# Addend rows of a graph attention layer by VectorE block transpose and two DMAs, with the output store, the values and the setup loads moved

## Chip, cores, metric

One core of one Trainium2 chip. The metric is the device time of that core in microseconds (us), as the median of the runs of one kernel. A single core has no second die to compare with, so a run counts as fast when it is within 1.5% of the fastest run of the same kernel.

## The reference, cut to what matters

64 graphs of 256 nodes, 256 features, fp32. Two layers:

```python
# layer 0: two graph attention (GAT) products, then a feed-forward
def _gat(h, adj, W, a, out_features):
    Wh = jnp.matmul(h, W)
    Wh1 = jnp.matmul(Wh, a[:out_features])
    Wh2 = jnp.matmul(Wh, a[out_features:])
    e = jax.nn.leaky_relu(Wh1 + jnp.swapaxes(Wh2, 1, 2), negative_slope=ALPHA)
    att = jax.nn.softmax(jnp.where(adj > 0, e, NEG), axis=1)
    return jnp.matmul(att, Wh)
h = _gat(_gat(x, adj, W1, a1, Fout), adj, W2, a2, W2.shape[1])
h = _layernorm(x + h, g_ln1, b_ln1)
x = _layernorm(h + relu(h @ w_ff1 + b_ff1) @ w_ff2 + b_ff2, g_ln2, b_ln2)
# layer 1: attention of 8 heads with 4 relations (a mask adj == r and values v_r each),
# output projection Wo, layernorm(x + ...), a feed-forward with gelu, layernorm
```

In each GAT product the sum of a column and a row vector goes through an exponential. The kernel exponentiates the two vectors instead, and needs the row vector (the *addend row*) on all 128 partitions.

## The kernel before

The 64 graphs are worked in 32 pairs. A pair is a Python generator that emits instructions and yields `(us, later, needs)`: how long TensorE's part takes, how much later the next step could go, and which stage it needs for itself. `in_turn` interleaves three pairs by these numbers while the program is built. So the order of instructions on each engine is fixed before the kernel runs.

The addend rows, by eight TensorE transposes (four per graph) and an eviction:

```python
def gat_weights(y, at, rise, ratio, adjT, empty, b):
    p = bank()
    for n in range(4):
        col = rise[:, n // 2, n % 2:n % 2 + 1]
        nc.tensor.transpose(p[:, n * P:(n + 1) * P], col.to_broadcast([P, P]), ident)
    up = work.tile([P, N], F32, name="up", bufs=2)
    nc.scalar.activation(up, p[:, :N], AF.Copy)
    ...                                   # e from p, up, adjT on VectorE; y scaled on ScalarE
```

What VectorE does after the output product of a pair's second GAT layer (the letter `h` further below):

```python
    add_rows(x, ps, b)                    # residual: one 128x512 addition
    layernorm(x, ln[0], b)                # statistics, two scalings per 128 rows
```

The head groups of the attention. A group is four heads of one graph, so a pair has four:

```python
    for n, (b, c) in enumerate(groups):
        ...
        sums(e, po); products(c, 0, v, e, po); products(c, 1, v, ms, po)
        if not last:
            e, ms = ahead, of_relation_1(groups[n + 1][0], ahead)    # VectorE: four masks
        divided(b, c, po)                 # VectorE: reciprocal, range check (junk), oT
        yield 3.1 if last else 4.1, 4.8 if last else 0.8, None
        if (b, c) == (0, KC - 1):         # after the second group
            v = values_tile()
            ...                           # values of the pair's second graph
        if n == 2:
            into_rows(0); yield 1.75, 0.0, None
    into_rows(1)                          # output projection of graph 1: needs the last oT
```

And the end of a pair:

```python
    yield from feed_forward(x, ff1, AF.Gelu, ln[3])
    nc.sync.dma_start(out[...], x)
    yield 3.44, 0.0, None
```

The setup loads pair 0 first, then the weights, and computes small corrections of the biases (matmuls with one column) before pair 0 begins.

## Time and profile before

| | before |
|---|---|
| time, median of the first 3 runs | 3408.89 us (3407.56 to 3410.56) |
| span in the profile | 3408.2 us |
| TensorE / VectorE / ScalarE busy | 98% / 55% / 40% |
| all waits of TensorE | 58.1 us |
| mean granted TensorE clock | 0.993 of full |

The second is where the last GAT product (L277) stands in TensorE's order of time before (start us, us, line, what, count):

```profile
346.64 3.62 PE L339 MATMUL ps<-w_L_gnn_W,ff 128*128 128x256 f32 x16
350.10 1.89 PE L277 MATMUL ps<-xw,e 128*128 128x256 f32 x8
351.82 3.62 PE L339 MATMUL ps<-w_L_gnn_W,ff 128*128 128x256 f32 x16
355.27 1.89 PE L277 MATMUL ps<-xw,e 128*128 128x256 f32 x8
357.00 7.07 PE L339 MATMUL ps<-w_L_gnn_W,ff 128*128 128x256 f32 x32
```

It stands between blocks of another pair's feed-forward (L339). The kernel before works through the GAT layers of three pairs, then through the attention of three pairs. VectorE is busy for 13.6 of the 19 us from 346 to 365 there, but no product of TensorE waits for it.

### The profile page before, as it was taken

To read this page: it belongs to the slowest core of one execution; us is meant where nothing else is said; L and a number is where in the kernel's file an instruction comes from. 1 tells how busy PE (TensorE), PEld (TensorE's weight loads), DVE (VectorE), ACT (ScalarE), POOL (GpSimd) and SP (SyncE) were. 2 spreads that over 40 slices of the span, in tenths; PEclk is the share of its full clock that TensorE was granted. 3 is DMA by queue.
4 is the path that set the end of the run, shared out by engine and by line. 5 is a ranking of instruction groups with operands and counts; after the bars stand their busy time and mean duration, and the time that the engine had idled before them with its cause. 6 is when DMAs were issued, how large, how long until landed. Compare 5 with 4: busy or idle time off the path is not lost.

```text
span 3408.2 us, 46925 instructions
## 1 busy us (share of the span) xinstructions
PE 3341.0 (98%) x18782; PEld 2172.0 (64%) x18782; DVE 1864.6 (55%) x4833; ACT 1366.7 (40%) x2576; POOL 202.9 (6%) x262
## 2 busy tenths in 40 slices
PE   5999999999999999999999999999999999999998
PEld 4666765675576667656756766676576567666755
DVE  3565465645645655656456556556564565565454
ACT  1424523443353255234433532552344335325432
POOL 0000000000000000000000000000000000000000
PEclk7999999999999999999999999999999999999999
DMA  5000100010010001000100100010011001000000
GB/s 162 7 13 25 38 7 7 27 36 7 13 38 19 13 26 38 7 7 30 33 7 13 38 19 13 26 37 7 7 32 31 7 13 38 19 7 19 13 1 14
DMA packets 67297, 78.19 MB, mean 23 GB/s; under 512 B 3713, under 2 KB 58113, under 8 KB 67073
## 3 DMA queue, kind: packets, MB, share of 16 engines
q1 hardware_dynamic: 67072, 75.13, 7.2%
q8 instruction: 150, 2.46, 0.3%
q14 instruction: 75, 0.61, 0.1%
HBM read 58.34 MB, written 16.78 MB: 22 GB/s over the span
## 4 chain that ended last, share of the span: by engine, by line
PE 94%; ACT 4%; DMA 1%; DVE 0%; SPq 0%; issue 0%; POOL 0%; POOLq 0%; DVEq 0%
PE ps L339 26%; PE ps L328 24%; PE ps L362 7%; PE ps L408 6%; PE ps L355 6%; PE ps L380 4%; PE ps L401 4%; PE ps L251 3%; PE ps L425 3%; PE ps L277 3%; PE ps L315 2%; PE ps L265 2%; ACT L213 2%; PE ps L223 1%; ACT L331 1%; ACT xw L267 1%
## 5 line engine op out<-in xcount | busy, mean ns | idle before, releaser
L317 ACT ACTIVATE yT<-ps 128x512 f32<-128x512 f32 x192 | 113.0, 589 | 1057.5 <-PE ps L315 1057.4
L328 PE MATMUL ps<-yT,w_L_gnn_w_ff 128*128 128x512 f32 x1024 | 478.3, 599 | 0.7 <-ACT yT L317 0.7
L328 PE MATMUL ps<-yT,w_L_gnn_W 128*128 128x512 f32 x1024 | 472.5, 596 | 1.4 <-ACT yT L317 1.4
L339 PE MATMUL ps<-w_L_gnn_w_ff,ff 128*128 128x256 f32 x2048 | 456.9, 381 | 0.0
L339 PE MATMUL ps<-w_L_gnn_W,ff 128*128 128x256 f32 x2048 | 456.8, 380 | 0.0
L339 PEld LDWEIGHTS ps<-w_L_gnn_W,ff 128*128 128x128 f32 x2048 | 389.1, 190 | 64.9 <-issue 14.6
L339 PEld LDWEIGHTS ps<-w_L_gnn_w_ff,ff 128*128 128x128 f32 x2048 | 388.0, 190 | 64.5 <-issue 14.3
L394 DVE TENSOR_TENSOR m<-a,adjT 128x512 f32<-128x512 f32 x512 | 327.5, 688 | 175.3 <-ACT a L385 131.1
L300 POOL TENSOR_TENSOR rstd<-rstd,mhalf 128x2 f32<-128x2 f32 x256 | 202.2, 790 | 3198.7 <-DVE rstd L299 3185.0
L385 ACT ACTIVATE a<-ps 128x512 f32<-128x512 f32 x512 | 264.3, 603 | 232.9 <-PE ps L380 232.7
L357 DVE TENSOR_TENSOR v<-ps,b_L_gnn_bv 128x512 f32<-128x512 f32 x128 | 88.2, 689 | 461.4 <-PE ps L355 461.4
L290 DVE TENSOR_TENSOR x<-ps,x 128x512 f32<-128x512 f32 x256 | 176.1, 688 | 262.6 <-PE ps L339 138.9
L331 ACT ACTIVATE ff<-ps,c_L_gnn_b_ff 128x512 f32<-128x512 f32 x256 | 175.9, 687 | 343.2 <-PE ps L328 343.2
L328 PEld LDWEIGHTS ps<-yT,w_L_gnn_W 128*128 128x128 f32 x1024 | 185.6, 190 | 178.7 <-issue 173.5
L328 PEld LDWEIGHTS ps<-yT,w_L_gnn_w_ff 128*128 128x128 f32 x1024 | 182.0, 190 | 177.8 <-issue 175.1
L355 PE MATMUL ps<-wv,yT 128*128 128x512 f32 x512 | 235.4, 592 | 0.0
L331 ACT ACTIVATE ff<-ps,c_L_gnn_b 128x512 f32<-128x512 f32 x256 | 175.7, 686 | 148.3 <-PE ps L328 146.7
L414 DVE RECIPROCAL s<-ps 128x256 f32<-128x256 f32 x128 | 224.2, 1751 | 0.0
L230 DVE SCALAR_TENSOR_TENSOR e<-ps,ratio,up 128x256 f32<-128x256 f32 x256 | 115.9, 477 | 172.6 <-ACT up L225 172.6
L297 DVE BATCH_NORM_STATS2 st<-x 128x6 f32<-128x256 f32 x512 | 192.8, 419 | 8.7
L355 PEld LDWEIGHTS ps<-wv,yT 128*128 128x128 f32 x512 | 97.5, 190 | 122.2 <-issue 122.2
L209 DVE TENSOR_REDUCE steep<-xw 128x1 f32<-128x4 f32 x128 | 19.8, 155 | 254.8 <-ACT xw L267 207.7
(96 smaller groups left out, 4047.9 us busy)
## 6 DMA issues: line engine op xcount, KB each, us to landing
xT<-in_xT SPq DMA_DIRECT2D x32, 512.0 KB, 4.5
adjT<-in_adjT SPq DMA_DIRECT2D x32, 512.0 KB, 3.8
x<-in_x SPq DMA_DIRECT2D x32, 512.0 KB, 4.2
out<-x SPq DMA_DIRECT2D x32, 512.0 KB, 3.2
w_L_gnn_w_ff<-in_L_gnn_w_ff SPq DMA_DIRECT2D x2, 1024.0 KB, 10.4
w_L_gnn_W<-in_L_gnn_W SPq DMA_DIRECT2D x2, 1024.0 KB, 6.9
wv<-in_L_gnn_Wv SPq DMA_DIRECT2D x2, 256.0 KB, 7.4
w_L_gnn_W1T<-in_L_gnn_W1T SPq DMA_DIRECT2D x1, 256.0 KB, 6.1
```

Of the source, the lines that this page charges most:

```text
L290: nc.vector.tensor_tensor(rows, p, rows, ALU.add)
L297: nc.vector.bn_stats(st[:, j, :], r[:, 2 * b + j, :])
L300: nc.gpsimd.tensor_tensor(rstd, rstd, mhalf[:, :2], ALU.pow)
L328: nc.tensor.matmul(p1, lhsT=w1[:, c, m * P:(m + 1) * P], rhs=yT[:, c, :], start=c == 0, stop=c == KC - 1)
L331: nc.scalar.activation(h, p1, func, bias=b1[:, m:m + 1])
L339: nc.tensor.matmul(p2[:, j * D:(j + 1) * D], lhsT=f[m][:, k * P:(k + 1) * P], rhs=w2[:, m, :], start=m == 0, stop=m == NF - 1)
L355: nc.tensor.matmul(ps, lhsT=yT[:, c, at:at + P], rhs=wv[:, c].rearrange("p r m -> p (r m)"), start=c == 0, stop=c == KC - 1)
L362: nc.tensor.matmul(ps, lhsT=w[:, d, c * P:(c + 1) * P], rhs=yT[:, d, :], start=d == 0, stop=d == KC - 1)
L385: nc.scalar.activation(a, ps[o], AF.Exp)
L394: nc.vector.tensor_tensor(m, a, adj, ALU.mult)
L408: nc.tensor.matmul(po[o * DH:(o + 1) * DH, :N], lhsT=v[:, jc, at:at + DH], rhs=ms[o][:, jc * N:(jc + 1) * N], start=r == 0 and jc == 0, st ...
L414: nc.vector.reciprocal(s, po[:, N:])
```

## The change

Its intent: take 512 transposes off TensorE, which is the bound. The addend columns of a pair are written 8 columns apart, transposed in 32x32 blocks by VectorE, stored to DRAM as 4 KB and loaded back onto all partitions as 512 KB. Around that, the schedule leaves more time for this trip; the second graph's values come after the first head group; a pair's output store comes 5 us later; the next pair's loads are asked for one GAT product later (`z` instead of `y` below); the setup loads come in order of need; and the small bias products move to the stage that uses them.

```diff
-        x = io.tile([P, 4, D], F32, name="x", bufs=4)
+        x = io.tile([P, 4, D], F32, name="x", bufs=5)
...
-    loaded = {0: load(0)}                # now after the weights of the first product
...                                       # bias products: relieve(...), called for pair 0 at each stage
-    def addends(y, at, layer, pair, b):
+    def addends(y, at, layer, pair):
...
+        blocks = small.tile([P, 2, 32], F32, name="blocks")
+        nc.vector.transpose(blocks.rearrange("p j c -> p (j c)"), rise.rearrange("p j c -> p (j c)"))
+        row = scratch.tile([2, 16, 32], F32, name="row")
+        nc.sync.dma_start(row.rearrange("j q c -> q j c"), blocks[0:P:8])
+        rows = work.tile([P, 8, 4, 32], F32, name="rows")
+        nc.sync.dma_start(rows.rearrange("p q n c -> p (q n c)"), row.rearrange("j q c -> (j q c)").partition_broadcast(P))
...
-            nc.tensor.transpose(p[:, n * P:(n + 1) * P], col.to_broadcast([P, P]), ident)
...                                       # twice, for the two GAT layers:
+        rows, ratio = addends(y, D + 2, 0, pair)
+        yield 1.75, 8.6, None
+        e = [gat_weights(y, D + 2, rows, ratio, adjT, empty, b) for b in range(2)]
+        yield 0.0, 4.6, None
...
-            if (b, c) == (0, KC - 1):
-                v = values_tile()
+            if n == 0:
+                following = values_tile()
...                                       # the values, then v = following after group 1
         yield from feed_forward(x, ff1, AF.Gelu, ln[3])
+        yield 3.44, 5.0, None
         nc.sync.dma_start(out[...], x)
-        yield 3.44, 0.0, None
```

More of the change, by code (lines that the diff above doesn't have):

```diff
@@ L78, in two_layers @@
     most = const.tile([P, NPAIR, 4], F32, name="most")
-    steep = const.tile([P, NPAIR, 4], F32, name="steep")
+    steep = const.tile([P, NPAIR, 2], F32, name="steep")
+    rises = [const.tile([P, 2, 32], F32, name=f"rise{n}") for n in range(2)]
+    for rise in rises:
+        nc.vector.memset(rise, 0.0)
     def weights(name, pool=const):
@@ L121, in two_layers, with layernorm_weights @@
             nc.vector.tensor_copy(w12[:, m], pw[:, :D + 4])
-    ln = [tuple(on_all(n, D) for n in names) for names in (
-        ("L0_gnn_g_ln1", "L0_gnn_b_ln1"), ("L0_gnn_g_ln2", "L0_gnn_b_ln2"),
-        ("L1_gnn_g1", "L1_gnn_beta1"), ("L1_gnn_g2", "L1_gnn_beta2"))]
+    loaded = {0: load(0)}
+    def layernorm_weights(g, beta, more=None):
+        return on_all(g, D), on_all(beta, D), more and (on_all(more, D), column(more + "c"))
+    ln = [layernorm_weights("L0_gnn_g_ln1", "L0_gnn_b_ln1", "L0_gnn_b_ff2")]
     ff0 = (weights("L0_gnn_w_ff1"), column("L0_gnn_b_ff1"), weights("L0_gnn_w_ff2"))
-    wq, wk, wo = weights("L1_gnn_Wq"), weights("L1_gnn_Wk"), weights("L1_gnn_Wo")
+    ln.append(layernorm_weights("L0_gnn_g_ln2", "L0_gnn_b_ln2", "L1_gnn_bo"))
+    wq, wk = weights("L1_gnn_Wq"), weights("L1_gnn_Wk")
     wv = const.tile([P, KC, 2, D], F32, name="wv")
@@ L133, in two_layers @@
     bq, bk, bv = column("L1_gnn_bq"), column("L1_gnn_bk"), on_all("L1_gnn_bv", 2 * D)
+    bqs = const.tile([P, KC], F32, name="bqs")
     nc.vector.tensor_tensor(bv[:, D:], bv[:, D:], bv[:, :D], ALU.subtract)
+    wo = weights("L1_gnn_Wo")
+    ln.append(layernorm_weights("L1_gnn_g1", "L1_gnn_beta1", "L1_gnn_b2"))
     ff1 = (weights("L1_gnn_W1"), column("L1_gnn_b1"), weights("L1_gnn_W2"))
-    bqs = const.tile([P, KC], F32, name="bqs")
-    with tc.tile_pool(name="setup", bufs=1) as setup, \
-            tc.tile_pool(name="psetup", bufs=2, space=bass.MemoryType.PSUM) as psetup:
-        for n, (name, readers) in enumerate((("L0_gnn_b_ff2", ((ff0[0], ff0[1]),)),
-                                             ("L1_gnn_bo", ((wq, bq), (wk, bk))),
-                                             ("L1_gnn_b2", ((ff1[0], ff1[1]),)))):
-            beta = ln[n][1]
-            nc.vector.tensor_tensor(beta, beta, on_all(name, D, setup), ALU.add)
-            b = setup.tile([P, KC], F32, name="c_" + name)
-            nc.sync.dma_start(b, t[name + "c"])
-            for w, bias in readers:
-                pw = psetup.tile([P, 512], F32, name="pw")
-                of = w.shape[-1] // P
-                for m in range(of):
-                    for c in range(KC):
-                        nc.tensor.matmul(pw[:, m:m + 1], lhsT=w[:, c, m * P:(m + 1) * P], rhs=b[:, c:c + 1],
-                                         start=c == 0, stop=c == KC - 1)
-                nc.vector.tensor_tensor(bias, bias, pw[:, :of], ALU.subtract)
-            if name == "L1_gnn_bo":
-                pw = psetup.tile([P, 512], F32, name="pw")
-                for c in range(KC):
-                    nc.tensor.matmul(pw, lhsT=b[:, c:c + 1].to_broadcast([P, P]),
-                                     rhs=wv[:, c].rearrange("p r m -> p (r m)"), start=c == 0, stop=c == KC - 1)
-                nc.vector.tensor_tensor(bv, bv, pw, ALU.subtract)
-        nc.vector.tensor_scalar(bqs, bq, SCALE, None, ALU.mult)
@@ L162, in two_layers @@
+    ln.append(layernorm_weights("L1_gnn_g2", "L1_gnn_beta2"))
+    for gbm in ln[:3]:
+        nc.vector.tensor_tensor(gbm[1], gbm[1], gbm[2][0], ALU.add)
     work = ctx.enter_context(tc.tile_pool(name="work", bufs=1))
     small = ctx.enter_context(tc.tile_pool(name="small", bufs=6))
+    scratch = ctx.enter_context(tc.tile_pool(name="scratch", bufs=4, space=bass.MemoryType.DRAM))
     psum = ctx.enter_context(tc.tile_pool(name="psum", bufs=8, space=bass.MemoryType.PSUM))
@@ L167, in bank, with relieve, relieve_attention @@
         return psum.tile([P, 512], F32, name="ps")
+    def relieve(bias, w, more):
+        p = bank()
+        of = w.shape[-1] // P
+        for m in range(of):
+            for c in range(KC):
+                nc.tensor.matmul(p[:, m:m + 1], lhsT=w[:, c, m * P:(m + 1) * P], rhs=more[1][:, c:c + 1],
+                                 start=c == 0, stop=c == KC - 1)
+        nc.vector.tensor_tensor(bias, bias, p[:, :of], ALU.subtract)
+    def relieve_attention(more):
+        relieve(bq, wq, more)
+        relieve(bk, wk, more)
+        nc.vector.tensor_scalar(bqs, bq, SCALE, None, ALU.mult)
+        p = bank()
+        for c in range(KC):
+            nc.tensor.matmul(p, lhsT=more[1][:, c:c + 1].to_broadcast([P, P]),
+                             rhs=wv[:, c].rearrange("p r m -> p (r m)"), start=c == 0, stop=c == KC - 1)
+        nc.vector.tensor_tensor(bv, bv, p, ALU.subtract)
     alone = {}
@@ L202, in of_graph, with gat_weights @@
         return slice(2 * b, 2 * b + 2)
-    def addends(y, at, layer, pair, b):
-        k = of_graph(b)
-        nc.vector.tensor_reduce(steep[:, pair, 2 * layer + b:2 * layer + b + 1], y[:, k, at:at + 2], axis=AX.XY,
-                                op=ALU.max, apply_absolute_value=True)
-        e1, e2 = y[:, k, at], y[:, k, at + 1]
-        rise, ratio = small.tile([P, 2, 2], F32, name="rise"), small.tile([P, 2], F32, name="ratio")
-        nc.scalar.activation(rise[:, 0], e1, AF.Exp, bias=shift[:, 0:1])
-        nc.scalar.activation(rise[:, 1], e1, AF.Exp, bias=shift[:, 0:1], scale=ALPHA)
-        nc.scalar.activation(ratio, e2, AF.Exp, scale=ALPHA - 1.0)
-        return rise, ratio
-    def gat_weights(y, at, rise, ratio, adjT, empty, b):
-        p = bank()
-        for n in range(4):
-            col = rise[:, n // 2, n % 2:n % 2 + 1]
-            nc.tensor.transpose(p[:, n * P:(n + 1) * P], col.to_broadcast([P, P]), ident)
-        up = work.tile([P, N], F32, name="up", bufs=2)
-        nc.scalar.activation(up, p[:, :N], AF.Copy)
+    def addends(y, at, layer, pair):
+        nc.vector.tensor_reduce(steep[:, pair, layer:layer + 1], y[:, :, at:at + 2], axis=AX.XY, op=ALU.max,
+                                apply_absolute_value=True)
+        rise, ratio = rises[layer], small.tile([P, 4], F32, name="ratio")
+        of_kind = rise.rearrange("p j (n s) -> p n j s", n=4)[:, :, :, 0]
+        for b in range(2):
+            e1 = y[:, of_graph(b), at]
+            nc.scalar.activation(of_kind[:, 2 * b], e1, AF.Exp, bias=shift[:, 0:1])
+            nc.scalar.activation(of_kind[:, 2 * b + 1], e1, AF.Exp, bias=shift[:, 0:1], scale=ALPHA)
+        nc.scalar.activation(ratio, y[:, :, at + 1], AF.Exp, scale=ALPHA - 1.0)
+        blocks = small.tile([P, 2, 32], F32, name="blocks")
[4 more added lines that the diff above has]
+        nc.sync.dma_start(rows.rearrange("p q n c -> p (q n c)"), row.rearrange("j q c -> (j q c)").partition_broadcast(P))
+        return rows, ratio
+    def gat_weights(y, at, rows, ratio, adjT, empty, b):
         e = work.tile([P, 2, N], F32, name="e", bufs=4)
@@ L229, in gat_weights @@
             k = 2 * b + j
-            nc.vector.scalar_tensor_tensor(e[:, j], p[:, N:], ratio[:, j:j + 1], up, op0=ALU.mult, op1=ALU.max)
+            nc.vector.scalar_tensor_tensor(e[:, j].rearrange("p (q c) -> p q c", q=8), rows[:, :, 2 * b + 1],
+                                           ratio[:, k:k + 1], rows[:, :, 2 * b], op0=ALU.mult, op1=ALU.max)
             nc.vector.scalar_tensor_tensor(e[:, j], adjT[:, k], empty[:, k:k + 1], e[:, j],
@@ L244, in gat_layers @@
         z = work.tile([P, 4, D + 4], F32, name="xw", bufs=2)
-        a, e = [], []
         for b in range(2):
@@ L253, in gat_layers @@
                 nc.scalar.activation(y[:, k], ps[:, :D + 4], AF.Copy)
-            a.append(addends(y, D + 2, 0, pair, b))
-            yield 1.75, b * 1.6, None
-        if pair + 1 < NPAIR:
-            loaded[pair + 1] = load(pair + 1)
-        for b in range(2):
-            e.append(gat_weights(y, D + 2, *a.pop(0), adjT, empty, b))
-            yield 0.5, b * 4.4, None
+            if b == 0:
+                yield 1.75, 0.0, None
+        rows, ratio = addends(y, D + 2, 0, pair)
+        yield 1.75, 8.6, None
+        e = [gat_weights(y, D + 2, rows, ratio, adjT, empty, b) for b in range(2)]
+        yield 0.0, 4.6, None
         for b in range(2):
@@ L267, in gat_layers @@
                 nc.scalar.activation(z[:, 2 * b + i, :D + 2], ps[:, :D + 2], AF.Copy)
-            a.append(addends(z, D, 1, pair, b))
-            yield 1.75, 0.4 + b * 0.6, None
-        for b in range(2):
-            e.append(gat_weights(z, D, *a.pop(0), adjT, empty, b))
-            yield 0.5, b * 4.4, None
+            if b == 0:
+                yield 1.75, 0.4, None
+        rows, ratio = addends(z, D, 1, pair)
+        if pair + 1 < NPAIR:
+            loaded[pair + 1] = load(pair + 1)
+        yield 1.75, 8.6, None
+        e += [gat_weights(z, D, rows, ratio, adjT, empty, b) for b in range(2)]
+        yield 0.0, 4.6, None
         for b in range(2):
@@ L292, in layernorm @@
     def layernorm(r, gb, b):
-        g, beta = gb
+        g, beta, _ = gb
         st, mv = small.tile([P, 2, 6], F32, name="st"), small.tile([P, 2, 2], F32, name="mv")
@@ L455, in attention @@
             yield 3.1 if last else 4.1, 4.8 if last else 0.8, None
-            if (b, c) == (0, KC - 1):
-                v = values_tile()
+            if n == 0:
+                following = values_tile()
                 for jc in range(2):
-                    values(v, jc, N + jc * P, yT)
+                    values(following, jc, N + jc * P, yT)
                     yield 1.72, 0.0, None
+            if n == 1:
+                v = following
             if n == 2:
@@ L471, in whole_way @@
         yield from gat_layers(pair, xT, adjT, x)
+        if pair == 0:
+            relieve(ff0[1], ff0[0], ln[0][2])
         yield from feed_forward(x, ff0, AF.Relu, ln[1])
         yield 3.44, 6.0, None
+        if pair == 0:
+            relieve_attention(ln[1][2])
         yield from attention(x, pair, adjT)
+        if pair == 0:
+            relieve(ff1[1], ff1[0], ln[2][2])
         yield from feed_forward(x, ff1, AF.Gelu, ln[3])
+        yield 3.44, 5.0, None
         nc.sync.dma_start(out[2 * pair:2 * pair + 2].rearrange("b (c p) d -> p (b c) d", p=P), x)
-        yield 3.44, 0.0, None
     in_turn((whole_way(pair) for pair in range(NPAIR)), 3)
-    ranges = ((reach, NPAIR * 4, N * SAFE), (most, NPAIR * 4, 1.0), (steep, NPAIR * 4, STEEP))
+    ranges = ((reach, NPAIR * 4, N * SAFE), (most, NPAIR * 4, 1.0), (steep, NPAIR * 2, STEEP))
     count = const.tile([P, len(ranges)], F32, name="count")
```

## The prediction

> **What bounds the kernel now.** I read the page's busy shares first, then TensorE's own waits, TensorE's groups by shape, the start in order of time, and one stretch in the middle.
>
> ```profile
> PE 3341.0 (98%) x18782; PEld 2172.0 (64%) x18782; DVE 1864.6 (55%) x4833; ACT 1366.7 (40%) x2576; POOL 202.9 (6%) x262
> ```
>
> TensorE is the bound and the others are near half. A busy share of 98% could hide waits, so the next view is who TensorE waited for (engine, line, releaser: us in total, times, longest):
>
> ```profile
> PE ps L223 <- ACT rise L213: 19.4, 23, 0.9
> PE pw L151 <- DMA b_L_gnn_bo<-in_L_gnn_bo: 18.9, 1, 18.9
> PE pw L119 <- DVE junk L113: 11.4, 1, 11.4
> PE ps L265 <- ACT xw L236: 2.9, 1, 2.9
> PE ps L277 <- ACT xw L236: 2.6, 1, 2.6
> ```
>
> All eight rows of that view add to 58.1 us in 3408. 30.3 of them are two waits at the start (L119, L151). The L265 and L277 waits are the first pair's, which has no company. From 78 us on, TensorE waits almost only for L223, the transposes that spread the addends; 20 of those waits are 0.92 us each, two in every batch of three pairs (ScalarE has just reloaded its table between Gelu and Exp). So the time is the sum of TensorE's own work plus the start, and only what leaves TensorE's queue counts.
>
> What L223 costs, from TensorE in order of time in the middle (start, us, line, what, count):
>
> ```profile
> 328.26 1.04 PE L223 MATMUL ps<-ident,rise 128*128 128x128 f32 x8
> 329.13 1.88 PE L328 MATMUL ps<-yT,w_L_gnn_W 128*128 128x512 f32 x4
> ```
>
> The 1.04 includes the pipeline's tail; the next group starts 0.87 us after the first. Eight transposes (one layer of one pair) hold TensorE for 0.87 us, 109 ns each, not the 273 ns that the group's mean shows.
>
> The start:
>
> ```profile
> 11.41 3.50 PE L119 MATMUL pw<-right,w_L_gnn_W1T 128*128 128x260 f32 x8 [11.41 <-DVE junk L113]
> ...
> 33.81 6.96 PE L151 MATMUL pw<-c_L_gnn_b_ff,w_L_gnn_w_ff 128*128 128x1 f32 x32 [18.90 <-DMA b_L_gnn_bo<-in_L_gnn_bo]
> ...
> 54.67 5.80 PE L251 MATMUL ps<-w,xT 128*128 128x260 f32 x16 [0.25 <-DVE c_L_gnn_b L153]
> ```
>
> The first useful product of pair 0 (L251) starts at 54.67 us although its own inputs are ready near 15.4 us (the second copy into w12 starts at 14.95 and takes 0.43). It is held behind the tiny bias products, 33.81 to 54.5 us, which wait for nearly all weights.
>
> **What the Trainium skill says.**
> 1. "TensorE: Matmul & The Clock Gate", Back-to-back issue gap: spacing, not duration, sets throughput; it gives about 81 ns per matmul of 128 columns. The trace agrees in kind, with 109 ns for these fp32 transposes beside a duration of 273 ns.
> 2. "DMA: Bandwidth & Descriptors", Anatomy of one DMA: a fixed cost of about 2 us plus bytes over 436 GB/s. For 512 KB that is an estimate of 3.2 us; the trace has 3.2 us (out), 3.8 (adjT) and 4.5 (xT). The page's fit is for the other descriptor path, but the sizes match here.
> 3. The same page, Two DMAs through the same engine are not ordered: a DMA that reads what another wrote must wait for its completion. So the new store and load cost two full latencies in series. No run yet shows it.
> 4. "VectorE: DVE Perf Modes", The three transpose paths: the VectorE transpose works in 32x32 blocks only. That is why the change spaces the columns and sends the row through DRAM. The trace before has no such instruction.
>
> **The change part by part.**
> *Transposes.* Removed: 32 pairs x 2 layers x 8 = 512 transposes on TensorE, 64 x 0.87 = 55.7 us, and their waits, 19.4 us. Both are on the path. Sum 75.1 us. Also removed: 128 ScalarE evictions of 0.38 us (49 us, beside other work, worth nothing).
> Added per pair and layer: one VectorE transpose of 128x64, taken as about 0.15 us as the small VectorE instructions are; a 4 KB store; a 512 KB broadcast load. 64 loads are 33.5 MB, at some 280 GB/s (what the start moves: 9.1 MB of loads in some 33 us) 120 us of DMA time spread over 3400: bandwidth is free. Latency is the question. From the end of a layer's products to the next matmul: eviction 0.39, two exponentials 0.58, VectorE transpose and hand-over 0.3, store 0.45 issue + about 2.0 (skill), load 0.4 + 3.8 (adjT row), two pairs of scalar_tensor_tensor 1.9, reciprocal 0.16, two scalings 0.9: 10.9 us, with one table load (1.28) 12.2. The schedule asks for 8.6 + 4.6 = 13.2 us of other work, more after rounding up to whole steps of 1.72 or 3.44 us. TensorE has it: while one pair is in these layers another is in a feed-forward (27.5 us of products: 8 x 1.72 + 4 x 3.44), and a third follows it. Now the two gaps are 7.6 and 10.4 us and cost only the 0.9 above. The slack is 1 to 3 us; the next pair's xT load (512 KB) becomes free exactly when the first layer's products end and can delay that layer's store by 2 us. I allow 8 us of new waits in all: some 10 batches, 0.8 us each.
> *Start.* The four setup loads no longer queue behind 1.5 MB of pair 0: at 280 GB/s 5 us, less some issue, so L119 can start near 7.5 and L251 near 12, 42 us earlier. But pair 0 now needs two store-and-load trips with nothing beside them, and the first queues behind the remaining loads, which the old kernel was issuing until 36.5 us. I estimate the first rows at 44 to 49 us, the second layer's products at 48 to 52, the third (L277) at 63 to 67 instead of 74.4. The 20.7 us of tiny products are not saved; they move. If they fall into the idle stretch of pair 0 the start gains some 8 to 12 us; if they stay after it in TensorE's order, the start loses about 10. VectorE's L240 for pair 3 runs at 61 us, far ahead of its place in the program, so instructions are moved forward when they can run: I give the first case 0.7. Expected gain 4 us.
> *Second graph's values earlier, x with five buffers, output store 5 us later.* No product is added or removed, and TensorE waits for none of these now: 0 us. They protect the queue that now carries the rows.
> Sum: 3408.9 - 75.1 - 4 + 8 = 3337.8; new waits are as likely near nothing, so I put the point at 3335.
>
> **The rivals.**
> *The DMA trip becomes the wait.* If a trip takes 3 us more than reckoned, every L265 or L277 in steady state waits some 1 to 2 us: 62 x 1.5 = 93 us, and the gain is gone (3400 or so). For it: the slack is thin, and stores, xT loads and rows now share one queue. Against it: transfers are only 7.2% of the engines' time, output stores of 512 KB land in 3.2 us, and the 8.6 looks fitted to such a trip. A weaker form, 20 us, gives 3350.
> *The start eats part.* Pair 0 alone pays two trips behind 9 MB of loads and the tiny products come later: +10 to +15 us instead of -4, so 3350.
> *VectorE or ScalarE as bound.* 55% and 40% busy, and ScalarE loses work: no.
> *Start goes well.* Rows sent before the prefetches, trips hidden: 20 us more, 3315.
>
> **Range and chances.** Removal of 75 us is firm; start (-20 to +15) and new waits (0 to 25) are not. Eight in ten: 3316 to 3360. 2% faster means under 3340.7, just above my point, so faster 0.57, within 2% 0.42, slower 0.01.
>
> **What would show it.** Right: no transpose group of L223's kind left and 18270 or so TensorE matmuls; TensorE's waits for the scaled rows (L265 and L277's successors) under 10 us after the start; the rows' load landing in about 4 us; L251's first start near 12 us. Wrong: waits of 1 us or more repeating at the same place of each batch, DVE waiting for the DMA of the rows for longer than the 13 us of cover, or the tiny products running after pair 0's L277 in time.

## More of the kernel before

TensorE's order in the traces was the order of the program.

The prediction shows most of what is to be read. Two more readings are needed for what follows. The first is the page's chain that ended last, before, as shares of the span:

```profile
PE 94%; ACT 4%; DMA 1%; DVE 0%; SPq 0%; issue 0%; POOL 0%; POOLq 0%; DVEq 0%
```

VectorE (DVE) has no part in it.

## The result and the profile after

A ratio below is the mean time of one kernel's fast runs over that of the other's in the same rounds, so it is not quite the ratio of the medians that stand beside it. Its interval is the 95% one.

| | before | after |
|---|---|---|
| time, median of 4 runs | 3408.22 us (3406.43 to 3410.56) | 3387.49 us (3387.21 to 3388.09) |
| ratio | | 0.994 [0.9925, 0.9955] |
| span in the profile | 3408.2 us | 3385.3 us |
| mean granted TensorE clock | 0.993 | 0.991 |

The change is 0.6% faster. The prediction said 3335 us, 3316 to 3360; the kernel is outside, on the slow side. The busy shares and the chain of the page after:

```profile
PE 3288.2 (97%) x18270; PEld 2108.3 (62%) x18270; DVE 1841.2 (54%) x4835; ACT 1262.0 (37%) x2326; POOL 203.1 (6%) x262
...
PE 83%; DVE 11%; DMA 3%; POOL 1%; issue 1%; ACT 0%; SPq 0%; POOLq 0%; DVEq 0%
```

The transposes are gone: 512 matmuls fewer, 18782 - 18270. The chain now runs through VectorE for 11% of the span, although VectorE's busy share fell from 55 to 54%. What TensorE waited for, after (engine, line, releaser: us in total, times, longest):

```profile
PE ps L437 <- DVE oT L430: 40.9, 30, 2.1
PE ps L274 <- ACT xw L247: 28.3, 1, 28.3
PE ps L289 <- ACT xw L247: 9.1, 1, 9.1
PE pw L121 <- DVE junk L115: 7.5, 1, 7.5
```

L274 and L289 are the GAT products that need the rows. Each waited once in the whole run, for pair 0. So the trip through DRAM is hidden in the steady state. The new wait is L437: the output projection waits for `oT`, the attention's divided result, once in nearly every pair. Neither instruction is in a changed line.

One such wait, after, in TensorE's order of time:

```profile
430.61 1.99 PE L289 MATMUL ps<-xw,e 128*128 128x256 f32 x8
...
441.73 1.05 PE L420 MATMUL ps<-m,v 128*32 128x256 f32 x16
442.71 0.66 PE L327 MATMUL ps<-ident,x 128*128 128x128 f32 x4
...
445.36 3.62 PE L351 MATMUL ps<-w_L_gnn_W,ff 128*128 128x256 f32 x16
448.81 0.59 PE L437 MATMUL ps<-w_L_gnn_Wo,oT 128*128 128x256 f32 x2
451.10 1.56 PE L437 MATMUL ps<-w_L_gnn_Wo,oT 128*128 128x256 f32 x6 [1.69 <-DVE oT L430]
```

The last head group's products end near 442.7. TensorE has 6.1 us of other work (442.71 to 448.81) before the output projection of graph 1 comes up, and stops after its first two matmuls. What VectorE did in that time, after, in order:

```profile
443.27 0.68 DVE L302 TENSOR_TENSOR x<-ps,x 128x512 f32<-128x512 f32 x1
...
444.97 1.22 DVE L251 TENSOR_REDUCE most<-adjT 128x4 f32<-128x1024 uint32 x1
...
447.69 0.88 DVE L318 SCALAR_TENSOR_TENSOR x<-x,rstd,b_L_gnn_beta 128x256 f32<-128x256 f32 x2 [0.58 <-POOL rstd L312]
448.49 1.75 DVE L426 RECIPROCAL s<-ps 128x256 f32<-128x256 f32 x1
...
450.63 0.42 DVE L430 TENSOR_TENSOR oT<-ps,s 128x256 f32<-128x256 f32 x1
```

The reciprocal of the last group (L426) had its inputs near 442.8; it starts at 448.49, 5.7 us later. Ahead of it in VectorE's queue stand the addition and layernorm of output projection 0, and a reduction of the next pair (L251). They themselves stand late, because earlier in the same attention VectorE had to do the addition and layernorm of both GAT products: L289 at 430.61 is the second of them, between head groups. The same place before, TensorE and VectorE in order of time:

```profile
306.52 7.17 PE L339 MATMUL ps<-w_L_gnn_W,ff 128*128 128x256 f32 x32
...
309.09 1.75 DVE L414 RECIPROCAL s<-ps 128x256 f32<-128x256 f32 x1
...
313.53 1.89 PE L425 MATMUL ps<-w_L_gnn_Wo,oT 128*128 128x256 f32 x8
```

There the last group's products end at 306.6 and the reciprocal starts 2.5 us later. TensorE has 7.0 us of other work (306.52 to 313.53), so the result, done at 311.65, is in time. The change adds 3.2 us to VectorE's delay and takes 0.9 us of work from in front of the projection.

The load of the two stretches, in one view: window, then busy us (instructions) of TensorE, its weight loads, VectorE, ScalarE and GpSimd, the granted clock, DMA share and GB/s. Both begin just before the first head group and end just after the last output projection. Before:

```profile
282.00:317.00 35.00, 35.00 (x313) 21.85 (x307) 26.15 (x52) 14.67 (x20) 1.58 (x2) 1.00 0.06 17
```

and after:

```profile
418.00:453.00 35.00, 33.31 (x315) 20.82 (x308) 29.51 (x64) 9.94 (x17) 2.38 (x3) 1.00 0.05 16
```

VectorE is busy for 26.15 of 35 us (75%) before, 29.51 us (84%) after. Over the whole run it is 55% and 54%: the average hides the place where TensorE waits. (The 60% in two expectations below is of 270 to 305 us before, which begins 12 us earlier in the attention; the like stretch after, 406 to 441, has 23.41 of 35 us, 67%.)

The order that does this, as matmul calls of one pair (read from the program; `y z h` GAT products: input, second, output; `F f` feed-forward first and second product; `q` projections, `v` values, `s` scores, `u p` sums and products of a head group, `o` output projection):

```
before, three pairs in turn through  y8 F8 z4 F2 z4 F6 f8 h4 f8 h4 f16,  then three through
        F10 q4 v2 s8 q4 v2 s8 u8 p16 F2 s8 u8 p16 F2 v4 s8 u8 p16 F2 o4 u8 p16 f16 o4 f16
after,  one pair at a time through
        q4 v2 s8 q4 v2 s8 u8 p16 h4 v4 s8 u8 p16 h4 s8 u8 p16 F2 o4 u8 p16 F2 f8 o4 f24
        F6 y8 F10 f16 z4 f8 z4 f8 F12
```

The `h4` that stood between feed-forward blocks stand between head groups now. The last output projection has `F2 f8` ahead of it instead of `f16`.

The start, after, all engines in order of time:

```profile
30.13 0.58 SPq L229 DMA_DIRECT2D row<-blocks  x1
36.60 0.34 SPq L231 DMA_DIRECT2D rows<-row  x1
...
43.96 6.37 PE L274 MATMUL ps<-xw,e 128*128 128x258 f32 x16 [28.33 <-ACT xw L247]
...
59.44 5.44 PE L289 MATMUL ps<-xw,e 128*128 128x256 f32 x16 [9.11 <-ACT xw L247]
...
68.22 3.63 PE L162 MATMUL ps<-c_L_gnn_b_ff2c,w_L_gnn_w_ff 128*128 128x1 f32 x32
...
73.52 10.37 PE L340 MATMUL ps<-yT,w_L_gnn_w_ff 128*128 128x512 f32 x20 [0.74 <-ACT yT L329]
```

Pair 0's first row was ready to store near 16.8 us, when its VectorE transpose ended; the store is issued at 30.13, after SyncE (SPq) has issued all remaining setup loads. Still, the first feed-forward product (L340) starts at 73.52, and at 85.66 before.

Where the 22.9 us between the two spans come from, by TensorE's time from one matmul's start to the next one's, with the waits counted apart:

| term | us |
|---|---|
| transposes gone, 61.2, and their waits, 19.4 | -80.6 |
| waits at the start: 11.4 + 18.9 before, 7.5 after | -22.8 |
| bias products: 20.6 before, 10.5 after | -10.1 |
| pair 0's waits for its rows: 28.3 + 9.1, against 2.9 + 2.6 | +31.9 |
| other matmuls, mostly the first product of layer 0's feed-forward (448.0 to 441.3) | -5.0 |
| GAT products spaced wider | +13.4 |
| L437: 40.9 of waits, and 9.4 to drain and refill | +50.3 |
| sum | -22.9 |

The rows of -5.0 and +13.4 belong together. Matmuls right behind a head group's narrow products are spaced wider. Before, these are feed-forward products (14.15 us for a pair's 32, against 13.74 where none of them stands there); after, GAT products (1.88 us for eight, against 1.73). The granted clock is 1.00 in both stretches above.

### The profile page after: what moved, and what is told of

Same layout as the page of the kernel before. It is cut to its first block, busy times and chain, and to the rows that moved or that the text cites. A ratio compares the mean times of both kernels' runs of the same rounds, so it can differ in the third digit from the quotient of the medians.

```text
span 3385.3 us, 45656 instructions
## 1 busy us (share of the span) xinstructions
PE 3288.2 (97%) x18270; PEld 2108.3 (62%) x18270; DVE 1841.2 (54%) x4835; ACT 1262.0 (37%) x2326; POOL 203.1 (6%) x262
## 3 DMA queue, kind: packets, MB, share of 16 engines
q1 hardware_dynamic: 79360, 108.95, 10.2%
## 4 chain that ended last, share of the span: by engine, by line
PE 83%; DVE 11%; DMA 3%; POOL 1%; issue 1%; ACT 0%; SPq 0%; POOLq 0%; DVEq 0%
PE ps L340 24%; PE ps L351 23%; PE ps L374 7%; PE ps L367 6%; PE ps L420 4%; PE ps L392 4%; PE ps L274 3%; PE ps L261 3%; DVE s L426 3%; PE ps L413 3%; PE ps L289 2%; DVE m L406 2%; DMA adjT<-in_adjT 2%; PE ps L327 2%; PE ps L437 2%; DVE x L318 2%
## 5 line engine op out<-in xcount | busy, mean ns | idle before, releaser
L340 PE MATMUL ps<-yT,w_L_gnn_W 128*128 128x512 f32 x1024 | 471.6, 597 | 0.7 <-ACT yT L329 0.7
L340 PE MATMUL ps<-yT,w_L_gnn_w_ff 128*128 128x512 f32 x1024 | 452.0, 594 | 0.7 <-ACT yT L329 0.7
L340 PEld LDWEIGHTS ps<-yT,w_L_gnn_w_ff 128*128 128x128 f32 x1024 | 192.6, 191 | 217.5 <-issue 207.7
L340 PEld LDWEIGHTS ps<-yT,w_L_gnn_W 128*128 128x128 f32 x1024 | 183.7, 190 | 185.7 <-issue 178.1
L240 DVE SCALAR_TENSOR_TENSOR e<-rows,ratio 128x256 f32<-128x256 f32 x256 | 116.1, 476 | 273.9 <-DMA rows<-row 249.4
L426 DVE RECIPROCAL s<-ps 128x256 f32<-128x256 f32 x128 | 223.6, 1747 | 0.0
L437 PE MATMUL ps<-w_L_gnn_Wo,oT 128*128 128x256 f32 x512 | 130.5, 389 | 40.9 <-DVE oT L430 40.9
```

The lines of the kernel that those rows point to most:

```text
L340: nc.tensor.matmul(p1, lhsT=w1[:, c, m * P:(m + 1) * P], rhs=yT[:, c, :], start=c == 0, stop=c == KC - 1)
L426: nc.vector.reciprocal(s, po[:, N:])
L437: nc.tensor.matmul(ps[:, j * D:(j + 1) * D], lhsT=oT[:, c, k * P:(k + 1) * P], rhs=wo[:, c, :], start=c == 0, stop=c == KC - 1)
```

## The experiments

The theory from the result, called A: the longer trip and the 5 us moved the GAT output products into the attention, VectorE falls behind there, and the last output projection pays. The rival B: moving the values behind the first group overloads VectorE, or makes the wait by its own order. Beside them stands the question of what the rows and the start are worth alone. Each kernel ran four times, in three sets of four kernels on one chip each; the kernel before had 7 runs in each set, with medians 3409.71, 3408.85 and 3410.45, so the sets can be compared to about a microsecond. All results were correct.

**1. values_back: the values at their old place.**

```diff
-            if n == 0:
-                following = values_tile()
+            if (b, c) == (0, KC - 1):
+                v = values_tile()
...
-            if n == 1:
-                v = following
```

> The changed kernel with the second graph's values put back behind the second head group. Theory A (the longer trips and the later end of a pair push the second layer's outputs h, with their residual add and layernorm on VectorE, between the head groups of the pair before; VectorE falls behind and the last output projection waits for oT): the order of h within the head groups stays, so some 30 waits of 1 to 2 us stay and the time is 3380 to 3395. Rival B (the values, 3.4 us of TensorE work that used to stand between the second and third head group, gave VectorE its breath, and moving them made the wait): the waits vanish and the time falls to 3335 to 3350.

Measured 3441.04 us (3438.47 to 3445.72), ratio 1.0097 [1.0081, 1.0114]. TensorE's largest wait there:

```profile
PE ps L420 <- DVE v L369: 66.1, 47, 2.4
```

B's forecast of a faster kernel falls: in this order the early values save 54 us (3441.0 - 3387.5). At the old place the values' bias additions queue up on VectorE behind the GAT layernorm, and the products wait for them. About half of the 54 us is this waiting (66.1 us against 40.9). The rest is in the products of the head groups, which take some 27 us more by the count of the account: after the waits the granted clock falls (0.76 from 439 to 446 us; over the run 0.981, against 0.991). The L437 wait is gone from the list; TensorE stops earlier, which gives VectorE time. So the values' place decides where TensorE stops, and B is right in that.

**2. store_back: the store at once, as before.**

```diff
-        yield 3.44, 5.0, None
         nc.sync.dma_start(out[...], x)
+        yield 3.44, 0.0, None
```

> The changed kernel with the output store issued at once and no 5 us delay at a pair's end. In the program's own order the pairs then go in batches of three again and no h stands between head groups. Theory A: TensorE's wait for oT falls from 40.9 us to under 10, VectorE's busy share inside the attention stretch falls from 84% to near 60%, time 3332 to 3350. Rival B: the values still stand early, so the waits stay and the time is over 3375. Rival C (the trips of the rows through DRAM cost TensorE time once their cover shrinks): new waits of L274 or L289 of 1 us and more per pair, time over 3360.

Measured 3372.76 us (3369.88 to 3374.97), ratio 0.9892 [0.9876, 0.9909]: 15 us better than after, between what A and B forecast. In the program's order the pairs go in batches of three again, and only one of three has its `h4` in the attention. That pair pays:

```profile
PE ps L437 <- DVE oT L430: 15.9, 10, 2.7
```

10 times, at most once per batch: 2.70 us four times, 0.96 us five times, 0.3 us once. So the late end is what brought the GAT products into *every* pair's attention; the longer trip alone brings them into one of three. I had taken the late end for the whole cause.

**3. cover: more time declared between the last head group and its output projection.**

```diff
-            yield 3.1 if last else 4.1, 4.8 if last else 0.8, None
+            yield 3.1 if last else 4.1, 8.0 if last else 0.8, None
```

> The changed kernel with 8.0 instead of 4.8 us asked for between the last head group and its output projection: one more feed-forward step (3.4 us) stands between, h stays between the head groups. Theory A and rival B alike: the wait for oT (1 to 2 us each) is covered, waits under 5 us, time 3335 to 3350. Rival D (the time is lost in something else, such as the switching of TensorE between small and full matmuls): the wait goes but the time falls by less than 20 us.

Measured 3344.88 us (3344.65 to 3348.45), ratio 0.9815 [0.9798, 0.9831]; the interval straddles 2%. The order differs from the kernel after only in that one feed-forward block more stands ahead of the last `o4` (`f16 o4 f16` for `f8 o4 f24`). In TensorE's order of time:

```profile
444.16 7.07 PE L351 MATMUL ps<-w_L_gnn_W,ff 128*128 128x256 f32 x32
451.07 1.89 PE L437 MATMUL ps<-w_L_gnn_Wo,oT 128*128 128x256 f32 x8
```

The eight matmuls of L437 run without a stop and the wait is gone from the whole list. It returns 42.6 us (3387.5 - 3344.9) of the 50.3 in the account; one new wait of 5.5 us at the end of the run (at 3301 us, where the last pair has no company) takes back most of the rest. VectorE's load in the same window is the same or higher, 30.46 of 35 us. The last reciprocal is as late as in the kernel after (5.6 us): its group's products end at 441.6, it starts at 447.17. So the 50 us are not a lack of VectorE time as such, but of 3.4 us of other work at one place. A and B expected this alike: the run shows what the wait costs, not what makes it. Rival D falls.

**4. rows_by_pe: the transposes back, the rest of the change kept.**

```diff
+        for n in range(4):
+            nc.tensor.transpose(p[:, n * P:(n + 1) * P], col.to_broadcast([P, P]), ident)
-        nc.sync.dma_start(row.rearrange("j q c -> q j c"), blocks[0:P:8])
-        nc.sync.dma_start(rows.rearrange("p q n c -> p (q n c)"), ...)
...                                       # and the yields of the GAT layers and the next pair's load as before
```

> The changed kernel with the addend rows made by the old TensorE transposes, all else as changed. Theory A: without trips the second layer is early enough, no h between head groups, no wait for oT (under 5 us), but 512 transposes are back (61 us of TensorE and some 18 us of waits): 3395 to 3408, so start and the rest alone gain 0 to 12 us against the kernel before. Rival B: the wait for oT stays (30 x 1.5 us) and the time is 3430 to 3450.

Measured 3374.85 us (3374.47 to 3376.63), ratio 0.9899 [0.9882, 0.9915]: 20 to 33 us faster than expected, and 12.6 us *faster than the whole change*. So within this change the new rows cost more than they save. The rest of the change gains 34 us without them: pair 0 has its transposes and no trip, and its first feed-forward product starts at 52.7 us.

**5. first_pe_cover: cover, and the transposes for pair 0 alone.**

```diff
+        if pair == 0:
+            return rise, ratio            # no trip
...
+        if by_transposes:                 # pair 0
+            for n in range(4):
+                nc.tensor.transpose(p[:, n * P:(n + 1) * P], rows[:, n % 2, at_n:at_n + 1].to_broadcast([P, P]), ident)
...
-            yield 3.1 if last else 4.1, 4.8 if last else 0.8, None
+            yield 3.1 if last else 4.1, 8.0 if last else 0.8, None
```

> The kernel with 8.0 us of cover, and pair 0 alone makes its addend rows by the old TensorE transposes; pairs 1 to 31 by the two DMAs. If the trips of pair 0 (behind the remaining loads, with nothing beside them) are what costs the start, TensorE's waits of 27.0 and 9.4 us before pair 0's second and third products shrink to some 3 us each, the first feed-forward product comes near 53 us instead of 74, and the time falls by 18 to 24 us from 3345, to 3320 to 3328. If the start is held by the loads of the weights instead, the time stays over 3338.

Measured 3320.68 us (3319.3 to 3323.83), ratio 0.9742 [0.9726, 0.9758]. This beats both kernels: 2.6% faster than before. Its start, TensorE in order of time:

```profile
22.36 3.75 PE L286 MATMUL ps<-xw,e 128*128 128x258 f32 x16 [2.63 <-ACT xw L259]
...
30.86 5.33 PE L301 MATMUL ps<-xw,e 128*128 128x256 f32 x16 [3.29 <-ACT xw L259]
...
47.55 10.55 PE L352 MATMUL ps<-yT,w_L_gnn_w_ff 128*128 128x512 f32 x20 [0.74 <-ACT yT L341]
```

The first feed-forward product starts 26 us earlier than after (73.52), and 24.2 us are gained over cover.

**6. more_dve: one spare 128x512 addition on VectorE after each GAT layernorm.**

```diff
             layernorm(x, ln[0], b)
+            spare = work.tile([P, 512], F32, name="spare")
+            nc.vector.tensor_tensor(spare, x[:, of_graph(b), :]..., x[:, of_graph(b), :]..., ALU.add)
```

> The changed kernel with one more VectorE addition of 128x512 (about 0.69 us, its result unused) after each graph's layernorm of the second layer, that is two per pair between the head groups; TensorE's order is unchanged. Theory A (VectorE's queue is the last to arrive at the output projection): the wait for oT grows by 1.0 to 1.4 us per pair, from 40.9 us to 70 to 85, time 3415 to 3430. Rival E (the wait is the latency of the last division alone, whatever VectorE did before): unchanged within 5 us, 3382 to 3392.

Measured 3445.84 us (3439.07 to 3448.65), ratio 1.0103 [1.0086, 1.0119]: 58 us slower than after, more than expected, although the L437 wait (here L440) grew less than expected, from 40.9 to 62.8 us. That is 22 of the 58. Most of the rest shows in TensorE's order of time:

```profile
454.56 0.59 PE L440 MATMUL ps<-w_L_gnn_Wo,oT 128*128 128x256 f32 x2
458.22 2.93 PE L440 MATMUL ps<-w_L_gnn_Wo,oT 128*128 128x256 f32 x6 [3.07 <-DVE oT L433]
```

The same six matmuls that took 1.56 us after a wait of 1.69 take 2.93 us after a wait of 3.07. The window after it, in the columns given above, has a granted clock of 0.61:

```profile
458.00:462.00 4.00, 3.78 (x11) 3.14 (x12) 0.94 (x3) 0.00 (x0) 0.00 (x0) 0.61 0.00 0
```

So a wait can cost its own time and then a stretch of 3.4 us at half the granted clock. That followed 14 of the 18 waits of over 2 us here. Between 80 and 3300 us such stretches add up to 51.2 us here and 10.2 us in the kernel after; half of the difference, some 20 us, is the loss (an estimate). A's direction is confirmed.

**7. rows_only: only the rows, in the kernel before.** The diff is the `addends`, `gat_weights` and GAT yields of the change, on the kernel before; nothing else.

```diff
-            nc.tensor.transpose(p[:, n * P:(n + 1) * P], col.to_broadcast([P, P]), ident)
+        nc.sync.dma_start(row.rearrange("j q c -> q j c"), blocks[0:P:8])
+        nc.sync.dma_start(rows.rearrange("p q n c -> p (q n c)"), ...)
...
+        yield 1.75, 8.6, None
```

> The kernel before with nothing changed but the addend rows (VectorE transpose, two DMAs, the delays that go with them); start, values, output store and buffers as before. In the program's order the pairs stay in batches of three and no h stands between head groups. Theory A: no wait of the large kind, at most one wait for oT in three pairs; of the 80 us of transposes and their waits some 18 are paid back in pair 0's two trips and some 25 in waits: 3370 to 3385. If the rows by DMA are no gain in themselves (rival C): over 3400.

Measured 3372.58 us (3371.17 to 3375.88), ratio 0.9894 [0.9877, 0.991], as expected. The rows alone gain 36 us of the 75 that I had reckoned. Pair 0's two trips wait 10.4 and 9.6 us there, and one pair of three has its `h4` in the attention.

**8. values_only: only the values early, in the kernel before.**

```diff
-            if (b, c) == (0, KC - 1):
-                v = values_tile()
+            if n == 0:
+                following = values_tile()
...
+            if n == 1:
+                v = following
```

> The kernel before with nothing changed but the second graph's values, moved behind the first head group. No h stands between head groups there, so VectorE is at 60% and neither place makes a wait: 3405 to 3412, no wait for oT or v of over 0.5 us. If the early values alone made the wait for oT: 3440 or more.

Measured 3409.05 us (3407.14 to 3410.23), ratio 0.9997 [0.9981, 1.0014]. In the old order the move is worth nothing, as the prediction said, and there is no wait for `oT`. Experiment 1 shows that this does not carry over to the new order.

**9. less_dve: the range check of the divided groups taken out.** The kernel guards itself with it; it is left out on purpose here. The results stay right for these inputs, but the guard is gone.

```diff
-            nc.vector.scalar_tensor_tensor(junk, po[:, N:], 1.0, s, op0=ALU.mult, op1=ALU.add,
-                                           accum_out=reach[:, pair, b * KC + c:b * KC + c + 1])
```

> The changed kernel without the range check that VectorE makes in each division (one scalar_tensor_tensor of 128x256 and its accumulator read, about 0.42 us in the queue, four per pair; the checked value is set to 1 once, so the guard is gone on purpose while the output stays right). TensorE's order is unchanged, h still stands between the head groups. Theory A: VectorE arrives 1.3 to 1.7 us earlier at the last division, the wait for oT falls from 40.9 us to under 8, time 3335 to 3350. If the wait were made by TensorE's order or by a DMA: unchanged, 3380 or more.

Measured 3358.19 us (3354.36 to 3360.1), ratio 0.9845 [0.9829, 0.9862]. The wait for `oT` fell to 15.5 us in 29 waits, from 40.9 in 30. Half a microsecond of VectorE work less per group returns 29 us: the direction of A again, with a gain smaller than expected.

**10. first_pe: the transposes for pair 0 alone, without cover.** The diff is that of experiment 5 without its last two lines.

> The changed kernel with pair 0's addend rows by TensorE transposes and nothing else: the start and the waits for oT are separate, so it gains what it gained beside the cover (24 us): 3360 to 3368, with the wait for oT still near 41 us.

Measured 3364.21 us (3358.98 to 3364.58), ratio 0.9861 [0.9844, 0.9877]. The start gains 23.3 us and the wait for `oT` stays, 40.6 us. The two repairs add up: 23.3 + 42.6 = 65.9, and both together gained 66.8 (3387.5 - 3320.7).

**11. start_only: only the order of loads and the bias products, in the kernel before.**

```diff
-    loaded = {0: load(0)}
...
+    loaded = {0: load(0)}                 # after the weights of the first product
...
+        if pair == 0:
+            relieve(ff0[1], ff0[0], ln[0][2])
...                                        # and so at the two other stages
```

> The kernel before with the changed start alone: loads in order of need, pair 0's loads behind the four setup loads, the tiny products in front of the stage that needs them; rows by TensorE transposes, values, output store and buffers as before. If the start alone is what made the kernel with the old transposes 35 us faster: 3370 to 3380. If the later output store had a part in it: 3385 or more.

Measured 3385.38 us (3385.01 to 3387.03), ratio 0.9929 [0.9913, 0.9946]. The start is worth 25 us when pair 0 need not make the trip; it alone does not make the 34 us of experiment 4 (the second case of the expectation). That leaves about 10 us of the 34 of experiment 4 for the rest. The traces put them mostly with the later end of a pair: TensorE's waits for the transposes are 19.4 us in 23 waits here and 10.2 in 13 in experiment 4. No run has the later end alone, so that share is a reading.

**12. store_values_back: rows and start, with values and store at their old places.** The diffs of 1 and 2 together.

> The changed kernel with the output store and the second graph's values both put back: the pairs go in batches of three, no h between head groups, and the values stand between the second and third group. It is the kernel with the rows alone (3372.6) plus the changed start, which is worth some 14 us beside pair 0's two trips (35 less 21): 3353 to 3364, waits for oT under 5 us. If the early values cost nothing in this order, as in the kernel before: the same as with the store alone put back, 3370 to 3376.

Measured 3359.71 us (3357.2 to 3362.86), ratio 0.9854 [0.9838, 0.9871], as expected. With it the four kernels that have the new rows and the new start make a table (medians, us):

| | values at the old place | values early |
|---|---|---|
| store at once | 3359.7 | 3372.8 |
| store 5 us later | 3441.0 | 3387.5 |

The later store costs 81 us or 15 us; the early values cost 13 us or save 54 us. Neither move has a worth of its own; each changes what stands in VectorE's queue when the other acts. With the store at once, the wait for `oT` is 15.9 us with early values and 1.5 us without: it takes both, the GAT products in the attention and the early values, for the stop to be at L437. Without both, this change would have been 28 us faster than it was.

## Why the prediction was wrong

**Transposes.** Right, and a little small: 75.1 us reckoned, 80.6 in the account. Eight of them took 0.96 us on average (61.2 / 64), not 0.87.

**The trip.** Right. The rows' load was to land in about 4 us and the row store in about 2:

```profile
rows<-row SPq DMA_DIRECT2D x64, 512.0 KB, 3.7
...
row<-blocks SPq DMA_DIRECT2D x64, 4.0 KB, 2.2
```

The VectorE transpose took 0.24 us; 0.15 was assumed. After pair 0 TensorE never waits for L274 or L289. The rival that feared most for this trip did not come about, and none of the 8 us allowed for new waits was of that kind.

**The skill's statements.** "DMA: Bandwidth & Descriptors", Anatomy of one DMA, gave an estimate of 3.2 us for 512 KB, by a fit for another descriptor path; measured 3.7. Two DMAs through the same engine are not ordered, of the same page, agrees: the load waited for the store's completion in each of its 64 uses, 113.2 us in all, 1.8 us each. "VectorE: DVE Perf Modes", The three transpose paths: the 32x32 blocks are why the columns stand apart, and that worked.

**The start.** Its sum was near, its parts were not. L121 at 7.50 and L261 at 11.86 came as reckoned. The rows' products came at 43.96 and 59.44, earlier than the 48 to 52 and 63 to 67 estimated. "Instructions are moved forward when they can run" did not hold on TensorE: the bias products stand where the program has them, at 68.22, after pair 0's L289. (On VectorE it did: pair 3's first instruction, L251, runs at 48.30.) This was the case to which the prediction gave 0.3 and a loss of 10 us. It cost less, because the bias products run at full clock now: 32 of them in 3.63 us at a granted clock of 1.00, against 6.96 us at 0.50 before. From the account the start and the trips sum to -22.8 - 10.1 + 31.9 = -1.0 us, and -4 was predicted; that the two are near is luck. A pair 0 without trips would have made it some 23 us better (experiment 10).

**The step that failed** is two sentences: "TensorE waits for none of these now: 0 us", for values, buffers and store, and "VectorE or ScalarE as bound. 55% and 40% busy, and ScalarE loses work: no". Also "while one pair is in these layers another is in a feed-forward" was read from the old order and taken for the new. The `yield` numbers that were to hide the trip, and the 5 us at the end of a pair, are inputs of a schedule that is laid out again from them. It put the GAT output products into the attention. There VectorE went from 75 to 84% busy, its last reciprocal started 5.7 instead of 2.5 us after its inputs, and one matmul group in nearly each pair waited 1.4 us on average (40.9 / 30). The wait and the refill are 50.3 us, and the spacing of the other products 13.4 - 5.0 = 8.4 more: 58.7 in place of the 8. The predicted sum with the measured terms is 3408.2 - 80.6 - 1.0 + 58.7 = 3385.3, the span of the profile. Two of the prediction's own signs of being wrong came true: waits that repeat at one place, and bias products after pair 0's L277 (now L289).

Shown by runs: the wait is worth 43 us and goes away with more work ahead of it (3); it grows and shrinks with VectorE's work (6, 9); the store's move is what brings it to every pair (2, 12). The early values decide that the stop is at L437 and not, longer, at L420 (1, 12). Only read from the traces: the wider spacing of the GAT products. Some of it is half clock in pair 0, where L274 and L289 follow long waits; the rest, roughly 0.3 us per pair where they follow the narrow products of a head group, was not tested. In the last third of the run the order shifts by one head group and the wait drops to about 1 us. There `F4 f8` stands ahead of the last `o4` instead of `F2 f8`, which fits A; no run tests it. Not tested either: the reciprocal further ahead in VectorE's queue, the fifth buffer of `x`, and the later place of the next pair's loads.

## What to carry to other kernels

A number in a static schedule is part of the program: before its effect is predicted, lay the order out again and look, stage by stage, at what stands in each engine's queue, because an engine at 54% over the run can be at 84% where another waits for it. When two moves act on the same queue, measure them together; alone, one of them was worth 0, and in the changed order 54 us. When a transfer replaces compute, keep the old way for the first tile, which has no company to hide the trip.

## What the Trainium skill lacked or had wrong

- "TensorE: Matmul & The Clock Gate", What's actually happening, ties the drop to half clock to an idle window of about 3.4 us. Here shorter waits were enough: after 3.07 us of waiting (experiment 6) six 128x256 matmuls took 2.93 us instead of 1.56, at a granted clock of 0.61, and in the kernel after a wait of 1.92 us (at 864.8) was followed by half clock. The length alone does not decide: 2.33 us at 564.1 and 3.18 us at 1834.5 in experiment 6, and three of four waits of 2.70 us in experiment 2, were followed by full clock. What else decides was not tested; one candidate is the quarter-width products that stand before these waits.
- "DMA: Bandwidth & Descriptors", Anatomy of one DMA, does not warn that a transfer of 2.2 us can wait far longer for its turn at the issuing engine. The first 4 KB row was ready near 16.8 us; SyncE, issuing the remaining setup loads one after the other, mostly 0.33 to 0.47 us each and one 3.33 us, came to it at 30.13.
- No page gives the time of a VectorE block transpose in fp32 of this shape: 128x64 took 0.24 us.
- No page says what an interleaved order can cost through the queue of a second engine: 5.7 us from ready to start for one reciprocal, against 2.5 before, and 50 us in the whole run.
